# Later issue positions for the state sums, gates and fronts in the first stage of a three-stage Mamba and window kernel

## The chip, the cores and the metric

The kernel runs on one core of one Trainium2 chip. The metric is the device time of one execution in microseconds (us), lower is better; it is taken as the median over several runs. The engines are named as in the profile: PE is TensorE (its weight loads are listed apart as PEld), DVE is VectorE, ACT is ScalarE, POOL is GpSimd, SP is SyncE, which here issues the DMAs.

## The reference, cut to what matters

Four layers follow each other. Only the first is touched by the change: two Mamba blocks over the same tokens (the second with the channels flipped), added to the normalised input.

```python
def _mamba(x, ...):                      # x: 4 x 4096 tokens x 192 channels
    xz = x @ in_w.T                      # to 2 x 384 channels
    xc, z = jnp.split(xz, 2, axis=-1)
    xc = silu(causal_conv4(xc))          # along the tokens
    dbl = xc @ x_w.T                     # 12 + 16 + 16 channels: dt, B, C
    dt = softplus(dt @ dt_w.T + dt_b)
    # for each of 384 channels and 16 states, along the tokens:
    #   h = exp(dt * A) * h + dt * x * B ;  y = sum over states of h * C
    y = (ys + D * xc) * silu(z)
    return y @ out_w.T
xs = _layernorm(x)
out = xs + _mamba(xs, m1...) + _mamba(flip(xs), m2...)
```

The second layer is one more Mamba block with a depthwise convolution and an MLP behind it; the third and fourth are a convolution with computed weights and a windowed product with an MLP.

## The kernel before, in words

The first layer is `two_mambas` (line 802), the second `mamba_block` (line 996), the third and fourth `conv_and_windows` (line 1209). The first two share the classes `Mamba` (line 419), `Scans` (line 694) and `Behind` (line 175).

**Units.** The tokens are cut into 32 tiles of 512. In the first stage each tile is a pair of units, one for each Mamba block. A unit has 12 state tiles k = 0 to 11 (`NQ`), each a tile `h` of 128 partitions by 4 groups of 512 tokens. Four state tiles (k % 4 = 0 to 3) make a chunk of 128 channels, so a unit has three chunks.

**The scan stream.** `Scans.run` (line 716) walks over all scans in order: step i is one DVE scan of 512 tokens (`Mamba.step`, line 634), 4 steps to a state tile, 48 to a unit, 96 to a pair. In step i it issues, in this order: at the first step of a state tile the loads of later rows on SP (`load`, line 588); the ACT exponential `dA` two steps ahead (`decay`, line 628, into 3 PSUM buffers); the scan; at a tile's last step the POOL read-out of `h` by C (`read`, line 645) and the DVE product that makes the next `h` (`product`, line 616). State tiles 3, 7 and 11 of the first stage (`shared`) have their product on POOL and live in `h_apart` (2 buffers); the others are in `h` (3 buffers). After that come the things that were put off to this step (`self.at`), and last one tick of the planner.

**What is put off.** With i the last step of state tile k: the PE sum over the states, `Mamba.sum` (line 653; 4 matmuls into the one PSUM tile `y`, and for k % 4 = 3 the skip matmul of line 668 too); then, once for each chunk, the DVE product of `y` with `z`, `skip` (line 677, `m_y` in the profile), which frees `y`; then `gated` (line 785), which tells that `z` is free and, after a pair's last chunk, adds the output projection `back` (line 877) to the planner. In the first stage the sum stood at i+6, the skip at i+8, the gate at i+8. `Mamba.gate` itself does nothing in the first stage.

**The planner.** `Behind` (line 175) holds four lanes of generators. Each `yield Piece(...)` says what the next piece costs and needs: PE us (`pe`, against a budget of 1.6 us per step), steps to wait (`wait`), flags that must be set (`after`), a PSUM bank (`bank`; 2 in all), ACT us (`act`, against 1.0 us per step), and `burst` for an activation that changes the ACT table, which is only issued at an edge: a step with i % 4 = 1 whose state tile isn't followed by one of `shared`. `later` (line 200) puts an eviction two steps behind its matmuls. The order on each engine is fixed when the program is built; on the chip each engine goes through its own list in order, and waits.

**Lane 1** has the fronts, one for each unit, one after the other (`Mamba.front`, line 462): three projections to `raw` (`ps_in`, line 474), the convolution as matmuls (`ps_conv`, line 548), the silu burst on `xc` (line 488), the product `ps_x` (line 492), `ps_dt` (line 503), the softplus burst on `dt` (line 512), the POOL product `dtx` (line 513), two DMAs to DRAM (line 518; from there the scans' rows are loaded), three projections to `z`, the silu burst on `z` (line 530). **Lane 3** has the layer norm of the following pair (`norm`, line 834): three sets of four ACT passes over `xs` (line 845) with small POOL operations between them (lines 849 and 853 to 855), then two transposes on PE (`ps_t`, line 863) and their evictions to `xT` (line 867). Lane 2 has `back`, lane 0 the spreads of C and B over the partitions (`ps_C`, `ps_Bs`, line 611).

`before` (line 914) runs at the first step of each unit: it loads the next tile's tokens, adds its norm, and adds the unit's front. `rows` must be there when the first load of a unit is due, some 8 to 12 steps ahead of its first scan; if it isn't, `force` issues pieces without regard to their waits.

Of the kernel before, what the change touches and what calls it, by code (L numbers as in the profile page):

```python
# [418 lines left out]
class Mamba:  # L419
# [42 lines left out]
    def front(self, xn, first, u):  # L462


        nc, K, behind = self.nc, self.taps, self.behind
        raw = self.work.tile([128, ND, K - 1 + T], F32, name="raw", bufs=1)
        if first:
            nc.gpsimd.memset(self.halo, 0.0)
        nc.gpsimd.tensor_copy(raw[:, :, 0 : K - 1], self.halo[:, :, : K - 1])

        def projected(e):
            ps = behind.bank([128, T], "ps_in")
            for k in range(2):
                nc.tensor.matmul(  # L474
                    ps, self.in_w[:, k, bass.ts(e, 128)], xn[:, k, :], start=(k == 0), stop=(k == 1)
                )
            return ps

        def project(e, to):
            ps = projected(e)  # L480
            return behind.later(lambda: nc.scalar.copy(to, ps))  # L481

        if self.summed:
            yield from self.sum_taps(raw, projected, u)
        else:
            yield from self.convolve(raw, project, u)
        xc = u["xc"]
        nc.scalar.activation(xc, xc, AF.Silu)  # L488
        yield Piece(2.6, bank=True, wait=2)
        ps = behind.bank([RK + 2 * NS, T], "ps_x")  # L490
        for d in range(ND):
            nc.tensor.matmul(ps, self.x_w[:, d, :], xc[:, d, :], start=(d == 0), stop=(d == ND - 1))  # L492
        dbl = u["dbl"] = self.work.tile([RK + 2 * NS, T], F32, name="dbl", bufs=2)
        h = behind.later(lambda ps=ps: nc.scalar.copy(dbl, ps))
        halves = []
        for d in range(ND):
            yield Piece(0.85, bank=True, after=[h], wait=0 if d else 3)
            if d == 0:
                dt = self.work.tile([128, ND, 1 + T if self.summed else T], F32, name="dt", bufs=1)
                dt = dt[:, :, :T]  # L500
                dtx = raw[:, :, K - 1 :]
            ps = behind.bank([128, T], "ps_dt")
            nc.tensor.matmul(ps, self.dt_w[:, bass.ts(d, 128)], dbl[:RK, :], start=True, stop=True)
            halves.append(
                behind.later(
                    lambda d=d, ps=ps: nc.scalar.activation(
                        dt[:, d, :], ps, AF.Identity, bias=self.dt_b[:, d : d + 1]
                    )
                )
            )  # L510
        yield Piece(after=halves, burst=True, act=4.1)
        nc.scalar.activation(dt, dt, AF.Softplus)
        nc.gpsimd.tensor_tensor(dtx, dt, xc, ALU.mult)
        rows = []
        for i, v in enumerate((dt, dtx)):
            yield Piece(wait=1 + i)
            r = self.dram.tile([DI, T], F32, name=("r_dt", "r_dtx")[i], bufs=3)
            nc.sync.dma_start(r.rearrange("(c p) t -> p c t", p=128), v)
            rows.append(r)
        yield Piece(1.7, bank=True, after=u["z_free"])  # L520
        u["rows"] = rows
        z = u["z"] = self.work.tile([128, ND, T], F32, name="z", bufs=2)
        made = []
        for d in range(ND):
            if d:
                yield Piece(1.7, bank=True)
            made.append(project(ND + d, z[:, d, :]))
        u["xn_read"] = True
        yield Piece(after=made, burst=True, act=4.1)
        nc.scalar.activation(z, z, AF.Silu)  # L530
        u["silu"] = True
# [162 lines left out]
class Scans:  # L694
# [21 lines left out]
    def run(self):  # L716
        n = len(self.units) * 4 * NQ
        m, u, _, _ = self.tile(0)
        self.behind.force(lambda: "rows" in u)
        for o in range(2):  # L720
            m.spread(u, o)
            self.behind.add(0, m.spread_C(u, o), Piece(0.85, bank=True))
        for i in range(2):
            m.load(u, 0, i)
        m.load(u, 1, 1)
        m.product(u, 0)
        for i in range(self.AHEAD):
            m.decay(u, 0, i)
        for i in range(n + 16):
            if i < n:  # L730
                self.step(i, n)
            for fn in self.due.pop(i, []):
                fn()
            self.behind.tick(self.edge(i + self.AHEAD, n))
        assert not self.due
# [5 lines left out]
    def step(self, i, n):  # L741
        m, u, k, j = self.tile(i)
        _, _, first, before, after = self.units[i // (4 * NQ)]
        if k == j == 0:
            if first:
                self.nc.vector.memset(m.state, 0.0)
            before()
        to = i + (12 if k % 2 else 8)
        if j == 0 and to < n:
            m2, u2, k2, _ = self.tile(to)  # L750
            self.behind.force(lambda: "rows" in u2)
            m2.load(u2, k2 // 2, k % 2)
        if i + self.AHEAD < n:
            m2, u2, k2, j2 = self.tile(i + self.AHEAD)
            m2.decay(u2, k2, j2)
        m.step(u, k, j)
        if j == 1 and k >= NQ - 2 and i + 8 < n:
            m2, u2, _, _ = self.tile(i + 8)
            m2.spread(u2, k - (NQ - 2))
            self.behind.budget -= 0.85  # L760
        if j == 2 and i + 6 < n:
            m2, u2, k2, _ = self.tile(i + 6)
            if k2 in m2.shared:
                self.behind.force(lambda: ("Bs", k2 % 2) in u2)
                m2.product(u2, k2)
        if j == 3:
            self.behind.force(lambda: ("C", k % 2) in u)
            m.read(u, k)
            if k >= NQ - 2 and i + 8 < n:
                m2, u2, _, _ = self.tile(i + 8)  # L770
                self.behind.add(0, m2.spread_C(u2, k - (NQ - 2)), Piece(0.85, bank=True))
            if i + 1 < n:
                m2, u2, k2, _ = self.tile(i + 1)
                if k2 not in m2.shared:
                    m2.product(u2, k2)
            late = 2 if m.shared else 0
            self.at(i + 4 + late, lambda: self.sum(m, u, k))
            if k % 4 == 3:
                c = k // 4
                self.at(i + 6 + late, lambda: self.skip(m, u, c))  # L780
                self.at(i + 8, lambda: m.gate(u, c))
                if c == ND - 1:
                    self.at(i + 8, lambda: self.gated(u, after))

    def gated(self, u, after):
        u["gated"][0] = True
# [15 lines left out]
def two_mambas(tc, x, gb_ap, m_ins, ex_aps, out, at_first):  # L802
# [3 lines left out]
    with ExitStack() as ctx:  # L806
# [14 lines left out]
        behind = Behind(psum, 1.6, 2, 3, 1.0)  # L821
# [9 lines left out]
            rows = x[u["b"], bass.ts(u["t"], T), :]  # L831
            nc.sync.dma_start(xt, rows.rearrange("(q p) c -> p q c", p=128))

        def norm(u):
            xt = u["x"]
            shift, rs = (work.tile([128, nq], F32, name=n) for n in ("shift", "rs"))
            xs = work.tile([128, nq, C], F32, name="xs", bufs=1)
# [19 lines left out]
            yield from passes(AF.Identity, scale=rs, bias=shift)  # L857
            xT = u["xT"] = work.tile([CP, 2, T], F32, name="xT", bufs=2)
            for k in range(2):
                yield Piece(1.1, bank=True, wait=1)  # L860
                ps = behind.bank([CP, T], "ps_t")
                for q in range(nq):
                    nc.tensor.transpose(
                        ps[:, bass.ts(q, 128)], xs[:, q, bass.ts(k, CP)], ident
                    )
                h = behind.later(
                    lambda k=k, ps=ps: nc.scalar.activation(
                        xT[:, k, :], ps, AF.Identity, scale=gb[:, k, 0:1], bias=gb[:, k, 1:2]
                    )
                )  # L870
# [3 lines left out]
        def front(u, i):  # L874
            yield from mambas[i].front(u["xT"], u["t"] == 0, u[i])
# [35 lines left out]
        for n, u in enumerate(units):  # L911
            following = units[n + 1] if n + 1 < len(units) else None

            def before(i, n=n, u=u, following=following):
                if i == 0 and following:
                    load(following)
                    last = [units[n - 1]["added"]] if n else []
                    behind.add(3, norm(following), Piece(wait=3, after=last))
                if following:
                    behind.add(1, front(following, i), Piece(after=[following["normed"]]))  # L920

            for i in range(2):
                stream.append(
                    (
                        mambas[i],
                        u[i],
                        u["t"] == 0,
                        lambda i=i, before=before: before(i),
                        (lambda u=u: behind.add(2, back(u), Piece())) if i else (lambda: None),
                    )  # L930
                )
# [899 lines left out]
```

## Time and profile before

| | us |
|---|---|
| median of 10 runs | 10769.93 |
| lowest and highest run | 10742.57, 10796.71 |
| the profiled execution's own time | 10796.71 |
| span of that execution (first to last instruction) | 10794.7 |
| first stage's scans, first to end of last | 77.1 to about 5404 |
| second stage's scans | 5505.9 to about 8863 |
| DVE busy from 77 to 5410 | 5038.12 of 5333.00 |
| POOL, PE, ACT busy in the same stretch | 4765.80, 4349.13, 3568.68 |
| granted PE clock there | 0.79 |
| DMA's mean busy share there | 0.65 |

Busy times are those of an engine's own instructions. A wait is the idle time right before an instruction, put down to what ended it. In a timeline, a row gives start, duration (first start to last end of the instructions merged in it), engine, line, operation, output and inputs, the count, and in brackets the idle time ahead of it with what ended it. PEclk is the share of full speed that the PE's clock was granted. A scan's listed duration (1.26 us) overlaps the next one's start; in a run of scans one takes 1.2 us.

### The profile page before, as it was taken

To read this page: it belongs to the slowest core of one execution; us is meant where nothing else is said; L and a number is where in the kernel's file an instruction comes from. 1 tells how busy PE (TensorE), PEld (TensorE's weight loads), DVE (VectorE), ACT (ScalarE), POOL (GpSimd) and SP (SyncE) were. 2 spreads that over 40 slices of the span, in tenths; PEclk is the share of its full clock that TensorE was granted. 3 is DMA by queue.
4 is the path that set the end of the run, shared out by engine and by line. 5 is a ranking of instruction groups with operands and counts; after the bars stand their busy time and mean duration, and the time that the engine had idled before them with its cause. 6 is when DMAs were issued, how large, how long until landed. Compare 5 with 4: busy or idle time off the path is not lost. (4 is left out here: it accounts for less than half of the span.)

```text
span 10794.7 us, 97520 instructions
## 1 busy us (share of the span) xinstructions
PE 9041.0 (84%) x30776; PEld 3525.9 (33%) x30776; DVE 9039.0 (84%) x7697; ACT 6651.2 (62%) x9626; POOL 7372.8 (68%) x3584
## 2 busy tenths in 40 slices
PE   7888888888888888888758999899899986889898
PEld 2222222222222222222223333333333333455455
DVE  7999999999999999999958888888888875555552
ACT  5666666666666666666646667676666653444433
POOL 6898888988889899888947777777676751111100
PEclk7787787787877878778767888888898887899999
DMA  6666666666666666666645555555555542112110
GB/s 168 172 183 177 174 170 173 182 174 170 175 177 175 175 175 180 171 175 179 163 113 147 142 140 146 140 146 142 139 148 136 146 113 71 43 49 63 43 40 18
DMA packets 969562, 1515.13 MB, mean 140 GB/s; under 512 B 244346, under 2 KB 277150, under 8 KB 968534
## 3 DMA queue, kind: packets, MB, share of 16 engines
q1 hardware_dynamic: 968190, 1505.85, 52.6%
q8 instruction: 245, 4.01, 0.2%
q10 hardware_dynamic: 856, 3.05, 0.1%
q14 instruction: 271, 2.22, 0.1%
HBM read 1295.45 MB, written 213.12 MB: 140 GB/s over the span
## 5 line engine op out<-in xcount | busy, mean ns | idle before, releaser
L636 DVE TENSOR_TENSOR_SCAN h<-dA,m_state,h 128x512 f32<-128x512 f32 x3840 | 4660.2, 1266 | 381.0 <-ACT dA L630 312.1
L649 POOL TENSOR_TENSOR h<-h,C 128x2048 f32<-128x2048 f32 x960 | 4348.4, 4530 | 77.3
L630 ACT ACTIVATE dA<-dtE,m_A 128x512 f32<-128x512 f32 x4608 | 3083.7, 685 | 1278.4 <-DVE h L636 1179.9
L623 DVE TENSOR_TENSOR h<-dtxE,B 128x2048 f32<-128x2048 f32 x960 | 2170.4, 2261 | 69.7 <-DMA dtxE<-r_dtx 69.7
L658 PE MATMUL y<-h,gather 128*32 128x512 f32 x7680 | 1263.1, 738 | 473.6 <-POOL h L649 281.7
L474 PE MATMUL ps_in<-xT,m_in_w 96*128 96x512 f32 x1536 | 1129.7, 880 | 192.0 <-ACT z L481 171.7
L1366 POOL TENSOR_TENSOR d<-d,rs 128x512 f32<-128x512 f32 x64 | 86.3, 1348 | 1600.7 <-DVE rs L1365 1580.1
L648 POOL COPY m_state<-h 128x4 f32<-128x4 f32 x960 | 181.1, 189 | 1169.6 <-DVE h L636 1143.6
L636 DVE TENSOR_TENSOR_SCAN h_apart<-dA,m_state,h_apart 128x512 f32<-128x512 f32 x768 | 924.9, 1260 | 47.7 <-ACT dA L630 47.5
L623 POOL TENSOR_TENSOR h_apart<-dtxE,Bs 128x2048 f32<-128x2048 f32 x192 | 892.7, 4649 | 43.6 <-ACT Bs L612 34.7
L649 POOL TENSOR_TENSOR h_apart<-h_apart,C 128x2048 f32<-128x2048 f32 x192 | 869.9, 4531 | 15.4
L548 PE MATMUL ps_conv<-raw,m_conv 128*128 128x512 f32 x1536 | 713.5, 607 | 0.0
L474 PEld LDWEIGHTS ps_in<-xT,m_in_w 96*128 96x128 f32 x1536 | 382.0, 272 | 955.2 <-issue 417.5
L1115 PE MATMUL ps_dw<-strip,dw 96*96 96x512 f32 x1152 | 590.6, 662 | 3.4 <-ACT x L1124 0.9
L658 PEld LDWEIGHTS y<-h,gather 128*32 128x32 f32 x7680 | 168.2, 117 | 1288.3 <-POOL h L649 558.2
L474 PE MATMUL ps_in<-xn,m_in_w 96*128 96x512 f32 x768 | 439.9, 717 | 164.6 <-ACT z L481 70.8
L492 PE MATMUL ps_x<-xc,m_pack 128*44 128x512 f32 x576 | 344.0, 746 | 228.0 <-ACT xc L488 189.3
L395 PE MATMUL ps_o<-hid,t 128*96 128x512 f32 x768 | 446.9, 729 | 75.9 <-ACT ln_rs L332 66.6
L1531 PE MATMUL sed_ps<-xn,sed 64*128 64x256 f32 (+3 forms) x2944 | 486.7, 404 | 7.0 <-DVE y L1550 7.0
L630 ACT ACT_TABLE_LOAD x345 | 442.6, 1283 | 14.7 <-DMA dtE<-r_dt 8.5
L548 PEld LDWEIGHTS ps_conv<-raw,m_conv 128*128 128x128 f32 x1536 | 284.8, 193 | 436.0 <-issue 347.7
L376 PE MATMUL ps_h<-xn,t 96*128 96x512 f32 x768 | 395.4, 662 | 30.3 <-ACT hid L381 16.7
(202 smaller groups left out, 12249.3 us busy)
## 6 DMA issues: line engine op xcount, KB each, us to landing
dtE<-r_dt SPq DMA_DIRECT2D x2304, 256.0 KB, 5.2
dtxE<-r_dtx SPq DMA_DIRECT2D x2304, 256.0 KB, 4.3
r_dt<-dt SPq DMA_DIRECT2D x96, 768.0 KB, 4.0
r_dtx<-raw SPq DMA_DIRECT2D x96, 768.0 KB, 6.4
x<-x SPq DMA_DIRECT2D x64, 384.0 KB, 3.8
img<-x SPq DMA_DIRECT2D x28, 512.0 KB, 9.2
xt<-in_x SPq DMA_DIRECT2D x32, 384.0 KB, 6.4
x<-o SPq DMA_DIRECT2D x32, 384.0 KB, 2.6
```

The costliest lines, as they stand in the source:

```text
L376: nc.tensor.matmul(ps, self.w1[:, k, bass.ts(m, 128)], x[:, k, :], start=(k == 0), stop=(k == 1))
L395: nc.tensor.matmul(ps, self.w2[:, m, bass.ts(k, CP)], h[:, m, :], start=(m == 0), stop=(m == NH - 1),)
L474: nc.tensor.matmul(ps, self.in_w[:, k, bass.ts(e, 128)], xn[:, k, :], start=(k == 0), stop=(k == 1))
L492: nc.tensor.matmul(ps, self.x_w[:, d, :], xc[:, d, :], start=(d == 0), stop=(d == ND - 1))
L548: nc.tensor.matmul(ps, self.conv[:, d, j, :], raw[:, d, j : j + T], start=(j == 0), stop=(j == K - 1))
L623: engine.tensor_tensor(h, u["rows", k // 2, 1], u[B, k % 2].unsqueeze(1).broadcast_to([128, 4, T]), ALU.mult)
L630: self.nc.scalar.activation(dA, u["rows", k // 2, 0][:, j, :], AF.Exp, scale=self.A[:, k, j : j + 1])
L636: self.nc.vector.tensor_tensor_scan(h[:, j, :], u.pop(("dA", k, j)), h[:, j, :], self.state[:, k, j : j + 1], ALU.mult, ALU.add,)
L649: nc.gpsimd.tensor_tensor(h, h, u["C", k % 2].unsqueeze(1).broadcast_to([128, 4, T]), ALU.mult)
L658: self.nc.tensor.matmul(u["ys"][32 * j : 32 * j + 32, :], self.ex.gather[:, i // 2, :], h[:, j, :], start=(i == 0), stop=(i == 3 and not s ...
L1115: nc.tensor.matmul(ps, dw[:, k, j, :], s[:, k, dy : dy + rows, dx : dx + HW], start=(j == 0), stop=(j == 8),)
L1531: nc.tensor.matmul(out, sed[p, int(h is not None), i ^ position(k, s), cols], xn[b, g][p, c, :], start=group(t) not in begun, stop=left[gr ...
```

## The change

In the first stage (`m.shared` not empty) the sum goes from i+6 to i+7, and to i+9 where k % 4 = 0, the first sum of a chunk; the skip goes from i+8 to i+10; the gate, with the `back` that it adds, from i+8 to i+10. The piece of `ps_x` waits 4 steps behind the silu burst in place of 2 (in the first stage only). The first piece of a front waits 2 steps. The norm no longer waits at its start for the `back` of the pair before it (`added`, which tells that `xT` was read); its two transposes wait for that in its place. The loop of `Scans.run` has 20 further rounds behind the last scan in place of 16, in both stages that use it. The second stage's positions (4, 6, 8) are those of before.

```diff
         xc = u["xc"]
         nc.scalar.activation(xc, xc, AF.Silu)
-        yield Piece(2.6, bank=True, wait=2)
+        yield Piece(2.6, bank=True, wait=2 if self.summed else 4)
...
-        for i in range(n + 16):
+        for i in range(n + 20):
...
-            late = 2 if m.shared else 0
-            self.at(i + 4 + late, lambda: self.sum(m, u, k))
+            added, skipped, gated = (7, 10, 10) if m.shared else (4, 6, 8)
+            if m.shared and k % 4 == 0:
+                added += 2
+            self.at(i + added, lambda: self.sum(m, u, k))
             if k % 4 == 3:
                 c = k // 4
-                self.at(i + 6 + late, lambda: self.skip(m, u, c))
-                self.at(i + 8, lambda: m.gate(u, c))
+                self.at(i + skipped, lambda: self.skip(m, u, c))
+                self.at(i + gated, lambda: m.gate(u, c))
                 if c == ND - 1:
-                    self.at(i + 8, lambda: self.gated(u, after))
+                    self.at(i + gated, lambda: self.gated(u, after))
...
-        def norm(u):
+        def norm(u, last=()):
...
             for k in range(2):
-                yield Piece(1.1, bank=True, wait=1)
+                yield Piece(1.1, bank=True, wait=1, after=last)
...
                     last = [units[n - 1]["added"]] if n else []
-                    behind.add(3, norm(following), Piece(wait=3, after=last))
+                    behind.add(3, norm(following, last), Piece(wait=3))
                 if following:
-                    behind.add(1, front(following, i), Piece(after=[following["normed"]]))
+                    behind.add(1, front(following, i), Piece(after=[following["normed"]], wait=2))
```

## The prediction

> **What bounds it now.** I read first the busy times of the stretch from 77 to 5410 us, the first stage's scans: DVE is busy 5038 of 5333 us, POOL 4766, PE 4349. So DVE sets the pace, and what is to be won there is its idle time. The waits of DVE from 0 to 5410 us say who ends it (total us, times, longest):
>
> ```profile
> DVE h L636 <- ACT dA L630: 110.9, 97, 8.0
> DVE m_y L681 <- PE y L668: 94.3, 32, 3.7
> DVE h_apart L636 <- ACT dA L630: 47.5, 61, 2.4
> ```
>
> These are 252.7 us, of which the scans wait 158.4 for a late exponential and the product with z waits 94.3 for a late sum. Nothing that the change does in this stage can win more, since the scans, products and skips themselves stay. Per pair of units (32 of them, 167.2 us each) it is 7.9 us.
>
> The timeline of DVE shows that the waits stand at the same places in each pair. I count steps s from a pair's first scan (0 to 95; this pair began at 2245.5, the next at 2412.7):
>
> ```profile
> 2345.88 0.69 DVE L681 TENSOR_TENSOR m_y<-y,z 128x512 f32<-128x512 f32 x1 [3.73 <-PE y L668]
> 2350.62 1.28 DVE L636 TENSOR_TENSOR_SCAN h<-dA,m_state,h 128x512 f32<-128x512 f32 x1 [0.51 <-ACT dA L630]
> 2354.05 3.63 DVE L636 TENSOR_TENSOR_SCAN h_apart<-dA,m_state,h_apart 128x512 f32<-128x512 f32 x3 [0.97 <-ACT dA L630]
> ...
> 2436.22 1.28 DVE L636 TENSOR_TENSOR_SCAN h_apart<-dA,m_state,h_apart 128x512 f32<-128x512 f32 x1 [0.57 <-ACT dA L630]
> ...
> 2468.74 4.81 DVE L636 TENSOR_TENSOR_SCAN h<-dA,m_state,h 128x512 f32<-128x512 f32 x4 [1.45 <-ACT dA L630]
> ```
>
> Place A is the skip of the first unit's last chunk at s = 55 (3.73); place B the two waits behind it, s = 59 and 61 (0.51 and 0.97); place C s = 15 and, 1.34 us, s = 16 of the next pair; place D s = 32 (1.45). Together 8.6 us.
>
> Then PE's timeline ahead of A and the granted clock (the columns end with PEclk, DMA share, GB/s):
>
> ```profile
> 2318.87 2.07 PE L611 MATMUL ps_C<-dbl,spread 44*128 44x512 f32 x2 [1.09 <-ACT xT L867]
> ...
> 2338.19 3.78 PE L474 MATMUL ps_in<-xT,m_in_w 96*128 96x512 f32 x4
> 2341.90 1.94 PE L658 MATMUL y<-h_apart,gather 128*32 128x512 f32 x8
> 2343.77 2.08 PE L668 MATMUL y<-xc,m_skip 128*128 128x512 f32 x2
> 2345.64 7.08 PE L548 MATMUL ps_conv<-raw,m_conv 128*128 128x512 f32 x16
> ```
>
> ```profile
> 2312.00:2318.00 6.00, 3.53 (x19) 1.19 (x17) 6.00 (x6) 2.83 (x6) 6.00 (x2) 1.00 1.06 255
> 2319.00:2345.00 26.00, 25.67 (x46) 6.87 (x47) 22.88 (x17) 17.35 (x25) 24.01 (x11) 0.50 0.61 162
> 2346.00:2360.00 14.00, 13.20 (x48) 4.66 (x46) 12.41 (x11) 6.86 (x11) 9.43 (x6) 1.00 0.46 121
> ```
>
> PE works 25.67 of 26 us at half clock: eight sum matmuls take 1.94 there and 1.07 in other places, a projection 3.78 against 1.98. It fell to half clock after the idle gaps of 0.46, 1.79 and 1.09 us from 2312 to 2319, in which it waited for the norm's passes, for DVE, and for the norm's eviction `xT`. So A and B are a PE backlog at half clock, opened by the norm.
>
> **The change, part by part.**
>
> *Skip and last sum (A).* The chunk's last sum was issued behind s = 53 and the skip behind s = 55: between them DVE does two scans (1.2 each) and one product (2.26), 4.66 us. It waited 3.73 more, so PE ended 8.4 us after the issue. Now the sum stands behind s = 54 and the skip behind s = 57: three scans and the product, 5.86 us. If PE is as late as before, the wait is 8.4 - 5.86 = 2.5 us, a gain of 1.2 of 3.7, or 30 of the 94 us; if PE isn't late, all 94 go. Below nothing: PE could be later still, since the front's matmuls now come ahead of the sum; its next piece after place A's sum is a convolution piece of two taps, 4 matmuls of 0.46, 1.8 us at full clock, so at worst +0.6 per pair (+19). I take a rest of 0.5 us per pair, a gain of 78, for what opened the backlog goes (next).
>
> *Norm.* It waited for `added`, and ran its passes at s = 18 to 38 (2444 to 2313 us, one pair apart), transposes at 39 and 40. Now it starts at s = 3: passes at 4 to 7, 12 to 15 hidden behind two POOL operations, and so on to s = 24, with the transposes behind `back`, near s = 25. No instruction is added. The cover for the earlier start is the load of `xt`: SP issued it at 2404.4 for a pair that began at 2412.7, it lands in 6.4 us, and the first pass comes near 2418, so some 7 us are spare; without them ACT would wait. What goes: ACT's waits for POOL inside the norm (1.45 and 2.48 us per pair), the pass of 0.63 us that sat inside the softplus burst at D (2466.17), and with both D itself: 1.45 x 32 = 46. Also the transposes' and `xT`'s part in PE's gaps ahead of A. And the silu burst on z at 2322.8, whose last input was evicted at 2309.9, was held over by the planner's ACT budget, which four norm passes of 0.55 were eating in just these steps; it may go to the edge at s = 37, eight steps earlier. What is late next: the passes now lie among the evictions of `back` and the silu burst at place C.
>
> *Fronts.* Behind that burst the front waits 2 steps, and `ps_x` 2 more. Lane 1 is full: fronts of the first unit from s = 45 to 85, of the second from 85 to 141. But most of it waits for edges: the last convolution eviction is at s = 61 and its burst at 65; `dt` is ready at 74 and its softplus at 77; in the second unit 101 and 109, 120 and 125. Two steps fit each time, in the tightest with one step to spare (76 for 77). So I cost them at nothing, hidden by the wait for the edge. If that cover is gone, a burst slips by one edge, 7.1 us (four scans and a product); the rows of `dtxE` are issued by 2396.7, land 4.2 us later, and their product starts at 2410.4, so about 9 us are spare: the first slip costs nothing, a second 5 us per unit. `ps_x` waited 5.6 us in each pair for its burst (the row PE ps_x <- ACT xc, 179.2 in 32); what stands behind it on PE's list is a sum, whose skip moves 2 steps later too.
>
> *B* goes as far as PE's backlog goes: 1.49 x 32 = 48 at most; I take two thirds, 32.
>
> *C.* ACT stood 1.20 and 1.49 us for `ps_out` ahead of the silu burst, because PE stood 2.71 us in the chunk's first sum, waiting for the skip. That sum now comes 3 steps later than it did and the skip 2, `back` 2 later; its evictions fall behind the burst. C is 1.91 us; a norm pass (0.63) now falls into the same burst, so I leave 0.6: 1.3 x 32 = 42 won. From both sides: 61 won, or nothing.
>
> *First sums.* PE waited 184.9 us for `m_y` in them, in 70 places; these waits shrink. But `h` has three buffers: the product behind s = i+12 writes into the one that this sum reads at i+9. It had six scans of room, now three, 3.6 us. Covered as long as PE isn't over 3.6 us late there (see the rivals).
>
> *Ends.* The four further rounds only move planner ticks between loops; in the second stage they delay the third's early work by four ticks. 0 to 8 us; I take 0. After the stage's last scan there is nothing left to overtake, and the 8.9 us of its last skip stay.
>
> *Sum:* 78 + 46 + 32 + 42 = 198 won. Against it I set 1 us per pair, 32, for new waits that no row of the old order shows, an eighth of the present ones. Net 166 us. The profiled execution took 10796.7 (span 10794.7 and 2.0 around it), so 10630.7, or -1.54%; it is the slowest of the ten runs, 0.25% over their median, and the same share of 10769.9 gives 10604 us.
>
> [...] The row: PE stood 2.49 us at 2303 and was at 0.50 from 2306 to 2309. [...]
>
> **Rivals.**
>
> *PE's lateness stays and takes another way (slower).* Speaks for it: half clock isn't due to the norm alone, 0.79 is the mean of the whole stretch. Then A wins only 30, B and C nothing, D 46; and the product at each chunk start meets a buffer still being read: the 8.4 us seen at A, less 3.6 of room, is 4.8 us per pair, +154. Net +78, 10848. It decides from 3.6 us of lateness on. Against it: PE is mostly early, and DVE has no wait for a buffer now.
>
> *Only the norm's part works.* D's 46 and A's 30, all else changes place: 10694.
>
> *All waits go.* 252.7 off: 10518.
>
> *It does nothing that shows.* The edges take up every delay, and the new order loses at C what it wins at D: 10750 to 10790.
>
> **How the numbers follow.** The forecast (10545 to 10660) 0.52; all waits gone 0.08; only the norm's part 0.12; no change 0.07; slower 0.21. The measurement can tell about 0.2% from no change. Faster by over 0.2%: 0.72; within: 0.07; slower: 0.21. The range goes from 10512 (all waits gone, with little around it) to 10830, which leaves out about half of the slower case. The likeliest case's own range is 10545 to 10660.
>
> **What would show it.** Right: `m_y` <- `y` under 30 us in the stage; no L845 <- POOL; no wait at s = 32; granted clock over 0.79; DVE over 96% busy from 77 us to the stage's end. Wrong: a wait of DVE L623 for PE's `y` (the buffer), `xs` waiting for the DMA of `xt`, or L623 for `dtxE` (fronts too late).

## The result and the profile after

| | before | after |
|---|---|---|
| median (runs) | 10767.58 us (32) | 10817.3 us (9) |
| lowest and highest | 10742.57, 10796.71 | 10809.9, 10829.51 |
| span of the profiled execution | 10794.7 | 10815.5 |
| start of the first stage's last `h_apart` scan | 5402.6 | 5434.3 |
| second stage's first scan | 5505.94 | 5536.91 |
| granted PE clock, first stage | 0.79 | 0.82 |

The ratio is 1.0049, 95% interval 1.004 to 1.0057: slower by about 50 us, where 166 us were forecast to be won. The profiled execution of before is the slowest of its runs (29 us over its median), so its own trace understates the loss: 20.8 us by the spans. The loss lies in the first stage (+31.7 us to its last scan). The second stage takes as long as before, and what stands behind the second stage's last scan is 10.2 us shorter (1931.4 us before, 1921.2 after).

The waits of DVE from 0 to 5440 us in the kernel after (total us, times, longest):

```profile
DVE h L623 <- PE y L658: 147.5, 61, 3.3
DVE h L636 <- ACT dA L630: 79.9, 98, 7.1
...
DVE m_y L681 <- PE ps_out L887: 19.0, 31, 3.5
...
DVE h_apart L636 <- ACT dA L630: 5.1, 4, 2.4
```

Against before, the wait of `m_y` for the sum, 94.3, is gone from the list but for the stage's end, and that of `h_apart` fell from 47.5 to 5.1. In their place stands a line that before did not have at all: the product (L623) waits 61 times for PE's `y`, that is for a sum that still reads the buffer it is to write. The four add up to 251.5 us; before's three were 252.7. So the change won what it aimed at and gave all of it back, and something more was lost than these waits show.

DVE's timeline over one pair (only its rows with a wait matter here) shows where:

```profile
2329.15 1.28 DVE L636 TENSOR_TENSOR_SCAN h<-dA,m_state,h 128x512 f32<-128x512 f32 x1 [0.60 <-ACT dA L630]
2333.95 2.46 DVE L636 TENSOR_TENSOR_SCAN h<-dA,m_state,h 128x512 f32<-128x512 f32 x2 [1.34 <-ACT dA L630]
2347.14 2.29 DVE L623 TENSOR_TENSOR h<-dtxE,B 128x2048 f32<-128x2048 f32 x1 [3.08 <-PE y L658]
...
2428.69 2.29 DVE L623 TENSOR_TENSOR h<-dtxE,B 128x2048 f32<-128x2048 f32 x1 [1.74 <-PE y L658]
2457.84 4.81 DVE L636 TENSOR_TENSOR_SCAN h<-dA,m_state,h 128x512 f32<-128x512 f32 x4 [0.29 <-ACT dA L630]
2475.04 0.69 DVE L681 TENSOR_TENSOR m_y<-y,z 128x512 f32<-128x512 f32 x1 [0.56 <-PE ps_out L887]
```

Place A (3.73), place B (0.51 and 0.97) and place D (1.45) have no wait any more; of place C's 1.91, 0.29 is left (the row at 2457.84). New are 3.08 and 1.74, one in each unit, at the product behind a unit's last scan (s = 47 and 95). It makes the next unit's first `h`, in the buffer that the sum of state tile k = 8 reads, the first sum of the unit's last chunk. Together 4.82 us per pair. The 0.60 and 1.34 stand at the silu burst on `z`, and 0.56 at a skip.

Where does the sum of k = 8 stand on PE? Before, it is issued in the same step as the first spread of B for the next unit (s = 41 or 89) and follows it at once; the front's third projection behind it waits 0.63 us (PE's timeline of before, at the end of a pair's second unit):

```profile
2400.77 1.12 PE L600 MATMUL B<-dbl,spread 44*128 44x512 f32 x2
2401.82 1.07 PE L658 MATMUL y<-h,gather 128*32 128x512 f32 x8
2403.51 1.98 PE L474 MATMUL ps_in<-xT,m_in_w 96*128 96x512 f32 x4 [0.63 <-ACT raw L481]
2405.43 1.12 PE L611 MATMUL ps_C<-dbl,spread 44*128 44x512 f32 x2
```

After, the sum is issued three steps behind that spread. The spread is followed by an idle PE, and the sum stands behind three other things, all at half speed (PE's timeline ahead of the wait of 3.08, a row of the windows over it, whose last three columns are PEclk, DMA share, GB/s, and ACT's timeline):

```profile
2333.32 1.12 PE L600 MATMUL B<-dbl,spread 44*128 44x512 f32 x2
2336.53 3.78 PE L474 MATMUL ps_in<-xT,m_in_w 96*128 96x512 f32 x4 [2.09 <-ACT raw L481]
2340.24 2.07 PE L611 MATMUL ps_C<-dbl,spread 44*128 44x512 f32 x2
2342.24 3.78 PE L548 MATMUL ps_conv<-raw,m_conv 128*128 128x512 f32 x4
2345.95 1.11 PE L658 MATMUL y<-h,gather 128*32 128x512 f32 x8
```

```profile
2336.00:2345.50 9.50, 8.97 (x10) 2.84 (x10) 8.05 (x8) 5.92 (x10) 8.02 (x6) 0.50 0.53 138
```

```profile
2330.43 1.49 ACT L530 ACTIVATE z<-z 128x1536 f32<-128x1536 f32 x1
...
2333.22 2.73 ACT L630 ACTIVATE dA<-dtE,m_A 128x512 f32<-128x512 f32 x4
2335.90 0.58 ACT L481 COPY raw<-ps_in 128x512 f32<-128x512 f32 x1
```

The front's third projection (`ps_in`) can't start until ACT has evicted its first to `raw`, since there are two banks, and ACT comes to that only behind the silu burst on `z` and four exponentials. PE idles 2.09 us, is granted 0.50 from 2335.86 to 2346.10, and the projection takes 3.78 for 1.98, the spread 2.07 for 1.12, the convolution piece 3.78 for 1.98. The sum ends at 2347.06, and the product starts at 2347.14.

What the waits don't show is DVE's own work. A skip behind a product, as before issued it, adds 0.40 us: product, skip and four scans take 7.495 from start to start in 100 undisturbed places of before, product and four scans alone 7.09. Between two scans, where the change puts it, it adds 0.59: 7.688 in 82 places of after, all between 7.68 and 7.69 (DVE's timeline of after; the next row's start closes the block):

```profile
5396.52 2.26 DVE L623 TENSOR_TENSOR h<-dtxE,B 128x2048 f32<-128x2048 f32 x1
5398.88 2.46 DVE L636 TENSOR_TENSOR_SCAN h<-dA,m_state,h 128x512 f32<-128x512 f32 x2
5401.26 0.67 DVE L681 TENSOR_TENSOR m_y<-y,z 128x512 f32<-128x512 f32 x1
5401.84 2.45 DVE L636 TENSOR_TENSOR_SCAN h<-dA,m_state,h 128x512 f32<-128x512 f32 x2
5404.20 4.79 DVE L636 TENSOR_TENSOR_SCAN h_apart<-dA,m_state,h_apart 128x512 f32<-128x512 f32 x4
```

0.19 us x 192 skips is 37 us, and that, with the waits equal (251.5 against 252.7), is the stage's 31.7 us to within 5.

### The profile page after: what moved, and what is told of

It reads as the page before. It is cut to its first block, busy times and chain, and to the rows that moved or that the text cites. A ratio compares the mean times of both kernels' runs of the same rounds, so it can differ in the third digit from the quotient of the medians.

```text
span 10815.5 us, 97361 instructions
## 1 busy us (share of the span) xinstructions
PE 8829.8 (82%) x30776; PEld 3451.7 (32%) x30776; DVE 9054.8 (84%) x7697; ACT 6654.6 (62%) x9626; POOL 7370.9 (68%) x3584
## 5 line engine op out<-in xcount | busy, mean ns | idle before, releaser
L623 DVE TENSOR_TENSOR h<-dtxE,B 128x2048 f32<-128x2048 f32 x960 | 2171.9, 2262 | 216.3 <-PE y L658 147.5
L658 PE MATMUL y<-h,gather 128*32 128x512 f32 x7680 | 1190.3, 705 | 410.8 <-DVE m_y L681 269.7
L474 PE MATMUL ps_in<-xT,m_in_w 96*128 96x512 f32 x1536 | 919.2, 740 | 472.4 <-ACT xT L869 196.5
L623 POOL TENSOR_TENSOR h_apart<-dtxE,Bs 128x2048 f32<-128x2048 f32 x192 | 893.7, 4655 | 7.3 <-ACT Bs L612 7.3
L649 POOL TENSOR_TENSOR h_apart<-h_apart,C 128x2048 f32<-128x2048 f32 x192 | 869.4, 4528 | 15.5
L548 PE MATMUL ps_conv<-raw,m_conv 128*128 128x512 f32 x1536 | 852.7, 690 | 0.0
L474 PEld LDWEIGHTS ps_in<-xT,m_in_w 96*128 96x128 f32 x1536 | 327.1, 228 | 1030.7 <-issue 306.6
L492 PE MATMUL ps_x<-xc,m_pack 128*44 128x512 f32 x576 | 384.8, 823 | 275.4 <-ACT o L904 149.0
L553 ACT ACTIVATE xc<-ps_conv,m_pack 128x512 f32<-128x512 f32 x192 | 132.2, 689 | 532.4 <-PE ps_conv L548 532.4
```

The source lines that it names most:

```text
L474: nc.tensor.matmul(ps, self.in_w[:, k, bass.ts(e, 128)], xn[:, k, :], start=(k == 0), stop=(k == 1))
L548: nc.tensor.matmul(ps, self.conv[:, d, j, :], raw[:, d, j : j + T], start=(j == 0), stop=(j == K - 1))
L623: engine.tensor_tensor(h, u["rows", k // 2, 1], u[B, k % 2].unsqueeze(1).broadcast_to([128, 4, T]), ALU.mult)
L649: nc.gpsimd.tensor_tensor(h, h, u["C", k % 2].unsqueeze(1).broadcast_to([128, 4, T]), ALU.mult)
L658: self.nc.tensor.matmul(u["ys"][32 * j : 32 * j + 32, :], self.ex.gather[:, i // 2, :], h[:, j, :], start=(i == 0), stop=(i == 3 and not s ...
```

## The experiments

The first three edit the kernel after; those named "norm" edit the kernel before with the norm's part of the change alone put in; the last group fills PE's gap. Ratios are to the kernel before on the same chip. No edit changes what is computed.

**One cause at a time, from the kernel after.** e1: a fourth buffer for `h`, paid for with single buffers for `xt` and `o`.

```diff
-            h = self.work.tile([128, 4, T], F32, name="h", bufs=3)
+            h = self.work.tile([128, 4, T], F32, name="h", bufs=4 if self.shared else 3)
```

> The changed kernel with four buffers for h in the first stage in place of three (one buffer in place of two for xt and o, to make room). The theory: the changed kernel's 147.5 us of DVE waiting for the chunk's first sum come only from the third buffer's reuse, so they go, and the time falls by 120 to 150 us, to 10670 to 10700. The rival: PE is late there whatever the buffers, and what is late behind it comes back as late exponentials; the time stays within 0.2% of 10817.

Measured 10804.06 us, ratio 1.0034 (1.0022 to 1.0047). The wait for the buffer is gone, and the time hardly moves:

```profile
DVE h L636 <- ACT dA L630: 193.0, 141, 8.5
DVE m_y L681 <- PE ps_out L887: 51.9, 29, 2.8
```

The exponentials, late by 79.9 us in after, are now late by 193.0. PE's order is the same (2.09 us idle, then 3.78, 2.07, 3.78), so what stands behind it comes late too: the scans wait 2.55 us for `dA` at 2182.50, five microseconds after that group. The third buffer is where the lateness showed, not its cause. (The single buffers of `xt` and `o` weren't tried alone; the longer wait of `m_y` for `ps_out` isn't theirs, since e9 below keeps both double and has 46.9.)

e2: the chunk's first sum at i+7 like the others (the two lines `if m.shared and k % 4 == 0: added += 2` left out).

> The changed kernel with the chunk's first sum at i+7, as the others, in place of i+9. The theory of the buffer: the reader of the buffer is issued two scans earlier, the product's wait falls from 4.8 us per pair to about 2.4, and the time by some 75 us to 10740. The rival: PE then stands in this sum until the skip one step before it has run, and what is behind it is late in turn; 10800 or more.

Measured 10806.65, ratio 1.0037 (1.0025 to 1.005). Again no wait for a buffer, and the exponentials late by 212.2. A chunk's first tile ends four steps behind the last tile of the chunk before; its sum at i+7 is thus issued one step past that chunk's skip at i+10, and stands on PE until the skip has freed `y`: PE waited 390.3 us for `m_y`, 269.7 in after.

e3: skip and gate back at i+8.

> The changed kernel with skip and gate at i+8 again (sums stay at i+7 and i+9). The theory that a skip between two scans costs DVE more than one behind the product (0.59 against 0.41 us in the two traces): 192 x 0.18 = 35 us less, 10782, and the wait of m_y for y stays under 40 us. The rival, that the later skip is what took away the wait of m_y for y: the 94 us come back, 10870.

Measured 10811.89, ratio 1.0042 (1.0029 to 1.0054): no different from after, and neither of the two expected times came. The costs of the later skip do go: `xT` no longer makes PE wait (196.5 us in after at `ps_in`, none here), nor do the exponentials at the silu on `z`. But the product's wait for the sum grows from 147.5 to 209.8. With all waits taken off, the stage of after is 33 us longer than that of before, and that of e3 7 us: so 26 us of DVE's own work go with the skip's old place, less than the 37 worked out above. `m_y` waits only 8.0 us for its sums in the stage although the skip is early again, so it wasn't the later skip that took A's wait away.

**One part at a time, from the kernel before.** e4: the norm alone.

```diff
-        def norm(u):
+        def norm(u, last=()):
...
-                yield Piece(1.1, bank=True, wait=1)
+                yield Piece(1.1, bank=True, wait=1, after=last)
...
-                    behind.add(3, norm(following), Piece(wait=3, after=last))
+                    behind.add(3, norm(following, last), Piece(wait=3))
```

> The kernel before with the norm's change alone (passes no longer wait for back, the transposes do). The theory of the prediction: the wait at step 32 goes (46 us) and part of PE's half-clock stretch ahead of the skip, so 10660 to 10720. The rival: the passes only meet other work in their new place, 10750 to 10790.

Measured 10683.1, ratio 0.9923 (0.9909 to 0.9937): this part alone wins 0.77%. The waits up to the last scan, at 5284.3:

```profile
DVE h L636 <- ACT dA L630: 96.7, 56, 8.1
DVE h_apart L636 <- ACT dA L630: 33.8, 38, 2.4
...
DVE m_y L681 <- PE y L668: 10.7, 21, 1.5
```

Places A, B and D are gone by the norm alone (94.3 to 10.7 for `m_y`). Of the 141.2 us left, 64.6 stand at place C (up to 1.04 and 1.78 us in a pair) and most of the rest at the starts and ends of units, 30.6 of it at the second scan of 16 pairs. And where PE idles, the sum comes directly behind the spread:

```profile
2267.14 1.12 PE L600 MATMUL B<-dbl,spread 44*128 44x512 f32 x2 [2.33 <-DVE h L623]
2268.19 1.93 PE L658 MATMUL y<-h,gather 128*32 128x512 f32 x8
2270.17 2.71 PE L474 MATMUL ps_in<-xT,m_in_w 96*128 96x512 f32 x4
2272.80 1.12 PE L611 MATMUL ps_C<-dbl,spread 44*128 44x512 f32 x2
```

PE is at half clock here too after 2.33 us of idling (the sum 1.93 for 1.07), but the sum comes first, so the product has no wait, and by the spread of C the clock is back.

e5, e10 and e11 add the sums' part to it: both moves; the chunk's first sum alone (i+9, the rest at i+6); all at i+7. As an example, e5:

```diff
-            self.at(i + 4 + late, lambda: self.sum(m, u, k))
+            added = (9 if k % 4 == 0 else 7) if m.shared else 4
+            self.at(i + added, lambda: self.sum(m, u, k))
```

> The norm's change and the later sums (i+7, chunk's first at i+9); skip, gate, fronts and ps_x as before. Of the 134 us between the norm alone (10683) and the whole change (10817), theory one, that the sums behind the front's matmuls meet the third buffer, puts most here: 10740 to 10800, with DVE's products waiting for y over 80 us. Theory two, that the later gate pushes the transposes against the softplus burst, puts little here: 10670 to 10700.

> The norm's change and only the chunk's first sum moved, to i+9 (the others at i+6, skip and gate at i+8). If the first sum's place does the harm of the later sums (170 us in the two together): 10820 to 10860. If the one step of the others does it: 10680 to 10710.

> The norm's change and all sums at i+7, the chunk's first too (skip and gate at i+8). If the first sum at i+9 does the harm: 10670 to 10710 here. If the one step of all does it: 10780 or more, with m_y waiting for y again.

| | us | ratio | product waits for `y` | scans wait for `dA` | `m_y` waits for `y` |
|---|---|---|---|---|---|
| e4, norm alone | 10683.1 | 0.9923 (0.9909 to 0.9937) | none | 130.5 | 10.7 |
| e5, sums at 7 and 9 | 10852.91 | 1.0083 (1.0071 to 1.0095) | 191.6 | 51.3 | 46.2 |
| e10, first at 9 | 10824.21 | 1.006 (1.0046 to 1.0074) | 207.4 | 58.4 | 15.5 |
| e11, all at 7 | 10818.58 | 1.0053 (1.0041 to 1.0066) | none | 186.1 | 72.7 |

The sums' part costs 1.6%, some 170 us, on top of the norm's gain, more than either theory of e5 had; it is the loss of the change. Either move does most of it alone: once the sum of k = 8 isn't between the spread of B and the third projection, it is late. At i+9 the product waits for it; at i+7 it comes in time for that, but PE's lateness reaches the exponentials, as in e1, and `m_y`.

e6: the norm, and skip and gate at i+10, with the sums left at i+6.

```diff
-                self.at(i + 6 + late, lambda: self.skip(m, u, c))
+                self.at(i + 6 + 2 * late, lambda: self.skip(m, u, c))
```

> The norm's change and skip and gate at i+10; sums at i+6 as before. Theory two: back, and with it the transposes, come two steps later and an xT eviction falls behind the softplus burst, so that the projections to z and the burst behind them are late (1.9 us per pair, 62 us), and a skip between scans costs 35 us: 10750 to 10790. Theory one: 10683 plus the 35 us, 10718.

Measured 10962.94, ratio 1.0186 (1.0173 to 1.0199), the slowest of all and far over both expectations. PE waits 599.0 us in the stage's sums for `m_y` (298.9 in e4): the next chunk's first sum is issued in the same step as the skip that it needs. So the later first sum is what the later skip asks for; the two can't be judged apart from each other on the way to i+10.

e7 and e8 add the fronts' waits to e4: `ps_x` at 4 steps; 2 steps ahead of a front.

> The norm's change and ps_x 4 steps behind its burst. The prediction's step, that the wait for the edge hides the two steps: 10683 within 0.2%. Against it: dt's last eviction misses an edge, or falls into a burst, and the time rises by 30 us or more.

> The norm's change and the front's first piece 2 steps later. The prediction's step, hidden by the wait for an edge: 10683 within 0.2%. Against it: the first projections come to stand among the sums and spreads of the unit's end, PE cools, and 30 us or more are lost at the chunk's last skip.

10681.96, ratio 0.9922 (0.9911 to 0.9934), and 10693.51, ratio 0.994 (0.9926 to 0.9953): neither can be told from e4.

With the later sums this is different. e3 is e5 with both of the fronts' waits and the loop's four further rounds, and it is 41 us faster (1.0083 to 1.0042). Some 10 us of that lie behind the second stage's last scan: every kernel with 20 rounds takes 1921 to 1925 us there, every one with 16 rounds 1931 to 1935, whatever else differs. The rest lies in the first stage (21 us by the traces), where the wait of `m_y` for its sums falls from 46.2 to 8.0. So the ratios lead from part to part: the norm 0.9923, with the sums 1.0083, with fronts and rounds 1.0042, with skip and gate 1.0049.

**Is it the clock?** e9 gives PE something to do in the gap: in the kernel after, the spread of B is written three times in the first stage, with the same values, for `o` = 0, which is the one ahead of the gap.

```diff
-        self.nc.tensor.matmul(B, self.ex.spread[:, o, :], u["dbl"], start=True, stop=True)
+        for _ in range(3 if self.shared and o == 0 else 1):
+            self.nc.tensor.matmul(B, self.ex.spread[:, o, :], u["dbl"], start=True, stop=True)
```

> The changed kernel with the spread matmul of the first B tile done three times over (the same result; 2.2 us more of PE work per unit, in the gap where PE waits for the eviction of raw). The theory of the clock: PE goes to half speed in that gap because the chunk's first sum no longer fills it; kept busy, the projection behind it takes 1.98 in place of 3.78, the convolution's first piece too, the sum comes some 4 us earlier, and the product's 4.8 us per pair go: 10660 to 10720. The rival, the order alone: the convolution stands ahead of the sum whatever the clock, and more work only makes PE later: 10817 or more.

Measured 10760.0, ratio 1.0001 (0.9992 to 1.001), between its two expectations: two useless matmuls more make the kernel half a percent faster. PE waits 14.1 us for `raw` in place of 110.9, and the product's wait falls from 147.5 to 65.6. Of the 63 us between the two traces 49 lie in the first stage; 14 lie in the second, where the edit does nothing, and were not explained. f1 puts the same edit into e5, f2 into e12 (below), f3 into e3.

> Norm freed and sums at i+7 and i+9 (10852.9 us before), plus two extra matmuls of the same spread of B in the first stage (2 x 0.5 us, the same values written again), so that PE doesn't idle 2.9 and 1.9 us ahead of the third ps_in. Theory clock (the sums cost because PE, idle in that gap, goes to half clock and is then late for the buffer): the product's wait for y falls from 191.6 to under 80 and the kernel to 10700-10770, most of the 170 us over the norm alone won back. Rival order (the sums stand behind too much work on PE, at whatever clock): the wait stays over 150 and the time over 10830; PE's extra 1 us may cost up to 30 more.

Measured 10770.4, ratio 0.9962 (0.995 to 0.9974). By the ratios, 1.2% under e5, three quarters of what the sums cost come back; by the times (82 us) and by the first stage in the two traces (5374.0 to 5299.6 us, 74 us) a little under half. The two differ because the kernel before took 10810.07 in this group of runs and 10763.96 in that of e5; no trace here shows why, so half is the safer figure. The product's wait falls from 191.6 to 97.0, 30 times for 61; under 80 were expected. Its PE timeline has both cases within 90 us of each other:

```profile
2223.26 3.86 PE L601 MATMUL B<-dbl,spread 44*128 44x512 f32 x6 [1.22 <-DVE h L624]
2227.05 3.78 PE L474 MATMUL ps_in<-xT,m_in_w 96*128 96x512 f32 x4
2230.76 2.07 PE L612 MATMUL ps_C<-dbl,spread 44*128 44x512 f32 x2
2232.76 3.78 PE L548 MATMUL ps_conv<-raw,m_conv 128*128 128x512 f32 x4
2236.47 1.94 PE L659 MATMUL y<-h,gather 128*32 128x512 f32 x8
...
2311.10 2.84 PE L601 MATMUL B<-dbl,spread 44*128 44x512 f32 x6
2314.03 1.98 PE L474 MATMUL ps_in<-xT,m_in_w 96*128 96x512 f32 x4
2315.94 1.12 PE L612 MATMUL ps_C<-dbl,spread 44*128 44x512 f32 x2
2316.99 1.98 PE L548 MATMUL ps_conv<-raw,m_conv 128*128 128x512 f32 x4
2318.91 1.07 PE L659 MATMUL y<-h,gather 128*32 128x512 f32 x8
```

The order is the same and PE doesn't idle between these rows in either. In the first, the clock falls during the spread (granted 1.00 from 2220 to 2224; the spread takes 3.86 for 2.84; 1.22 us of idling ahead, and 2.44 some ten microseconds earlier, both in its PE timeline): 13.2 us from the spread's start to the sum's, and the product behind it waits 3.94. In the second it is 7.8 us and there is no wait. Sorting all such places by the time of the projection:

| | places with the projection over 2.5 us | mean wait of the product there | other places | mean wait there |
|---|---|---|---|---|
| e5 | 61 | 3.14 | 1 | 0 |
| f1 | 30 | 3.23 | 32 | 0 |
| e9 | 19 | 3.45 | 43 | 0 |
| f3 | 52 | 3.37 | 10 | 0 |

Not one warm place has a wait, and each cold place has one. In f1 the cold places are all second units of a pair, so there the unit could be the reason; in e9 both units have both (14 cold and 17 warm first units, 5 and 26 second ones), and in f3 too (25 and 6, 27 and 4). (In after itself 31 places are cold, mean 3.08, and in the other 30 the clock falls within the group: 2.07 to 2.47 for the projection, then 3.78 for the convolution, and 1.74 of wait.) So in the new order the buffer's wait is due to the half clock. Half clock alone doesn't make it: in before 34 of the same 62 places are cold, and none has a wait. It takes the later place of the sum and the half clock together.

> The best version (norm starts without a wait, sums, skips and gates where they were before; 10627.6 us) plus the same two extra matmuls. There the first sum still fills PE's gap. Theory clock: little cold time is left in that gap, so the extra matmuls only stand in the way of the sum: 10620-10660, no better. Rival (half clock costs there too): under 10600, with the exponentials' waits of 71 us cut in half.

Measured 10713.98, ratio 0.991 (0.9898 to 0.9923), slower than the same without them (0.9875; the first stage of its trace is 95 us longer) and than expected: where the sum itself stands behind the spread, the extra matmuls come ahead of it and cost more than they keep.

> The whole change with skip and gate back at i+8 (10811.9 us), plus the two extra matmuls. If the clock behind the gap, and the skip's and gate's shift, are two separate costs of the change, both go here: 10690-10740, under the 10760.0 that the extra matmuls reached on the whole change. If the shift of skip and gate cost nothing: 10750-10770. If the gap's clock is not what made product wait: over 10790.

Measured 10797.05, ratio 0.9987 (0.9979 to 0.9996). The expectation of 10690 to 10740 failed: the intervals of e9 and f3 overlap, and the filler keeps only 10 of 62 places warm here, 43 in e9. What keeps PE warm ahead of the gap in the one and not in the other wasn't found. f3 is f1 with the fronts' waits and the rounds, and 27 us slower, where e3 was 41 us faster than e5: what these waits are worth changes its sign with what stands around them. Nor is the later skip's and gate's price settled by itself: it is at most small in total, since what it costs at `xT` and on DVE comes back at the buffer.

**A better version.** e12: e4 with the norm's first wait, 3 steps, left out too.

```diff
-                    behind.add(3, norm(following, last), Piece(wait=3))
+                    behind.add(3, norm(following, last), Piece())
```

> The norm's change, and the norm started three steps earlier still (no wait behind its load), so that its second set of passes is through before the silu burst at step 13. The wait of 1.04 and 1.78 us per pair at that burst (90 us over the stage) should fall by half or more: 10620 to 10650. The rival: the first passes wait for the load of xt, and ACT's exponentials with them: 10683 or more.

Measured 10627.6 us, ratio 0.9875 (0.9862 to 0.9889), the fastest of all. Up to its last scan (5227.1):

```profile
DVE h L636 <- ACT dA L630: 45.6, 56, 2.4
DVE h_apart L636 <- ACT dA L630: 25.7, 36, 1.8
```

With 7.9 for `m_y` that is 79.2 us, 62.0 less than e4, and its stage ends 57.2 earlier.

## Why the prediction was wrong

It forecast 10604; it got 10817.3, and the slower rival's mechanism.

*The step that failed is "First sums".* It said: "Covered as long as PE isn't over 3.6 us late there", and set against the rival that "PE is mostly early, and DVE has no wait for a buffer now". PE was over 3.6 us late at 61 of the 63 units that have a next one, 6.7 us (3.6 of room and 3.08 of wait) in the one shown. PE was early enough in the old order because the sum stood directly behind the spread of B. The step looked at the room that DVE leaves the sum, and not at what PE has ahead of it in the new place: an idle gap for `raw`, a projection, a spread and a convolution piece. At full clock these last three take 1.98 + 1.12 + 1.98 = 5.1 us and f1 shows that this fits; at half clock they take 9.6. Nor did it see that the sum itself kept the gap short: before, PE waited 20.3 us for `raw`, after, 110.9.

*The rival's price was right, its accounting only in part.* It had 4.8 us per pair for the buffer; 3.08 + 1.74 = 4.82 was measured, 147.5 in all against 154. That is in part luck: its 4.8 was one lateness carried over from place A, and the measured figure is two waits at other places, behind a gap that it didn't have. And it let A win only 30 and B and C nothing, and all three came in; it had none of the skips' 37 us nor of the other new waits (below). That its 10848 is only 31 us off comes from terms that cancel, the 10 us won behind the second stage among them.

*A, B, C, D.* All four places were emptied (of C, 0.29 is left) as predicted. A and B were credited to the wrong part, though. The norm alone (e4) takes away A, B and D; it was given D's 46 us and won about 84. C it leaves. That one goes with the later sums, as the prediction had it, but without the later skip: 64.6 us in e4, 15.9 in e10, where only the chunk's first sum was moved. The prediction said as much in "what opened the backlog goes"; the later sums and skips, which it put A under, were not needed for A. The rival "Only norm's part works", 10694, is what e4 measured within 11 us, as a kernel of its own; its terms weren't right either, since A, B and D all went and new waits came at the units' starts and ends. The premise that the norm opened the backlog held for A; it did not hold for half clock in general: at all 61 places of after where the product waits, PE idles 0.84 to 2.09 us ahead of the third projection, and the clock falls to 0.50 between 0.77 us before that projection's start and 1.77 us behind it.

*Fronts.* Costed at nothing, and with the sums in their old places (e7 and e8) nothing shows; with the later sums (e3 against e5) they win 20 to 30 us. *Ends.* Put at 0, or 8 lost; behind the second stage's last scan 10.2 us were won. Of the change's edits only the loop's rounds reach that far; they weren't tried alone.

*New waits, 32 us.* The rest of the new waits, without the buffer's, is the 0.60, 1.34 and 0.56 shown, 17.5, 40.2 and 19.0 us in the stage, 77 where 32 was put. The first two come through the gate: `back` and with it the norm's transposes come two steps later, the second eviction of `xT` falls behind the softplus burst, and PE waits 6.28 us for it at 2487.84; in e3, with the gate at i+8, both are gone.

*Unseen:* the skip's 26 to 37 us on DVE. A step that is moved was priced by what it waits for and not by its neighbours on its own engine.

*Its signs.* Right as listed: `m_y` <- `y` gone, no L845 <- POOL, no wait at s = 32, clock 0.82. All of these hold in a kernel that is slower. DVE busy over 96% failed (5052.47 of 5364 us, 94.2%), and the first sign of "wrong", L623 waiting for `y`, is the first line of the waits.

*Half clock.* A gap of 2.09 us was enough for it at 2336 in after, and the clock fell 1.4 us into it. The prediction looked at half clock ahead of A and behind the gap of 2.49 us at 2303, and not at the sums' new place.

## What to carry to other kernels

When work is moved later on an engine, ask what it was filling: on PE a small matmul in a gap can keep the clock up for what stands behind it (with two more in it, the projection stayed under 2.5 us at 32 of 62 places in f1, at 1 in e5). Two useless matmuls there were worth half a percent in e9, and lost time in f2 (0.9875 to 0.991), where a useful one stood in that place already. Count for each moved instruction what will stand ahead of it in its new place, at the slow clock as well as the fast one (3.78 and 1.98 us for a projection here), and price it between its new neighbours. Try the parts of a change alone: one of this change's parts was a clear gain that another hid.

## What the runs showed of the hardware

- PE fell to 0.50 after gaps of 2.09 us (after, 2336) and 2.33 us (e4, 2267), and in f1 after one of 1.22 us with one of 2.44 some ten microseconds before it. In f1 it stayed there up to the end of the sum at 2238.41, though PE doesn't idle from the spread on (3.78, 2.07, 3.78 and 1.94 for 1.98, 1.12, 1.98 and 1.07), while in e4 it was back at the spread of C, 5.7 us behind the gap (1.93 for the sum, 2.71 for the projection, then 1.12). What tells the two apart was not found.
- In the traces of before and after the granted clock is 1.00 or 0.50, and its 767 and 837 changes all lie whole multiples of 3.413 us apart (in after 2318.79, 2325.62, 2335.86, 2346.10, 2366.58). In the stretch of 3.41 us ahead of a fall PE was busy for 0.33 and 0.31 of the time at the median of the first stage (from 0 up to 0.94 and 1.00), ahead of a return to full clock for 0.90 or more and 0.80 or more. What decides a fall was not found.
- The same elementwise instruction of 128 x 512 costs DVE 0.40 us behind another elementwise one (before, 7.495 against 7.09) and 0.59 between two scans (after, 7.688 against 7.09), though the trace lists 0.67 to 0.69 for both. What makes the difference was not shown.
